# Fc1 of a conditional-experts kernel: one level of the seven-product form for one row, or two levels for two rows with streamed weights

## The chip, the cores and the metric

One core of a Trainium2 chip (trn2) runs the whole kernel. The metric is the device time of one execution in microseconds. A TensorE instruction on fp32 data appears in the profile as two "passes", so one matmul in the code is two matmul instructions in the counts.

## The reference, cut to what matters

```
x: [16, 512, 512]                     # 16 batch rows b, 512 positions, 512 features
h  = gelu(x @ fc1_w.T + fc1_b)        # [16, 512, 2048]
y  = [h @ fc2_w.T + fc2_b  (384 outputs, shared),
      h @ experts_w[idx[b]].T + experts_b[idx[b]]  (128 outputs, one expert for each row)]
x1 = x + y
a  = tanh(x1 @ W1 + b1)               # [16, 512, 128]
s  = a @ v                            # one score for each position
p  = softmax over l of s[l], masked by the row's type: l <= j, l >= j, or l != j
out[j] = x1[j] + (sum over l of p[j, l] x1[l]) / (number of l allowed)
```

## The kernel before, in words

Everything is fp32 and lies transposed: features or hidden units on the 128 partitions, positions along the free axis. A row is split into two halves of 256 positions (HC).

fc1 and fc2 use the seven-product block form: a 2 x 2 block product is made from seven products of sums of blocks. The sums of weight blocks are called s1 to s4, those of the moving side xs (for x) or t1 and in-place sums in hT. Products are called p1 to p7, and the same numbers are the names that fc2 passes to `at(...)`.

- fc1 of a row b is four groups g (`Group`); a group makes 7 products, each of 2 output tiles m and 2 depth chunks k, so 4 matmuls of 128x128 by 128x256. Accumulators are PSUM banks bx, ba, bd and by. After each product one operation on ScalarE (ACT: L294, L300, the Gelu at L285) or on VectorE (DVE: L305, L314) takes its result.
- The 7 weight pieces of a group have two sets of buffers (`pw`, 14 buffers of 256 KB). For the first row the sums are made on DVE and stored to DRAM (`w1s`); later rows load the pieces with SP's queue.
- fc2 of a row is seven products of 16 matmuls (`fc2`). Its shared weights stay in SBUF (fc2_sb, fc2_lo and the sums fc2s); the row's expert is gathered by POOL (GpSimd) and its sums (exs) are made on DVE.
- Then comes `Pooling(b)`: the projection and tanh (L461, L465), the scores (L470), small softmax steps on 32 partitions, coefficients that go to DRAM and come back broadcast (cb), and for each of four chunks of 128 features: weigh (u = x1T times c1), a reversed copy of u on ACT, recur (the scan f at L714), two passes on ACT (v), and finish (two DVE operations into x1T). At last `flip` transposes each chunk into yo (two buffers) and stores it.

The order is written out by hand: each engine executes in the order in which the Python code emits. Pooling of row b runs as a generator beside fc1 and fc2 of row b + 1. Each `yield t` is a cost in us; `slot(budget)` goes on until the budget is used. A negative `yield -n` ends the call and makes the next n - 1 calls of slot do nothing. In fc2, `at("1")`, `at("1b")`, `at("2")` give budgets, `at("5")` runs what is left ("drains"), and `at("7")` and `at("6")` emit two flips each. A name stands behind the emission of the product that it names.

What ends a row in fc2, with the line numbers of the profile:

```
            product(bd, of("a22"), b21, KH, add=True)
            at("4")
            add(out_block(1, 0), bd, u21, ALU.add)     # L387
```

The next row's projection reads all of x1T, so it waits for that add.

Of the kernel before, what the change touches and what calls it, by code (L numbers as in the profile page):

```python
# [17 lines left out]
def tile_cond_experts_then_prompt_pool(  # L18
# [29 lines left out]

    HC = S // 2
    KD = ND // 2  # L50
    KH = NH // 2
    MW = 2 * P
    NG = HID // 2 // MW
    assert NS == 3 and PART == P and ND == 4
# [3 lines left out]
    pw = ctx.enter_context(tc.tile_pool(name="pw", bufs=2 * 7))  # L58
    ps_m = ctx.enter_context(tc.tile_pool(name="ps_m", bufs=1, space=bass.MemoryType.PSUM))
    ps_y = ctx.enter_context(tc.tile_pool(name="ps_y", bufs=1, space=bass.MemoryType.PSUM))  # L60
    ps_l = ctx.enter_context(tc.tile_pool(name="ps_l", bufs=2, space=bass.MemoryType.PSUM))
# [3 lines left out]
    NAMES = ("a11", "a12", "a22", "s1", "s2", "s3", "s4")  # L65
    SUMS = ("s1", "s2", "s3", "s4")
    w1s = {(g, n): dram.tile([P, KD, MW], F32, name=f"w1s_{g}_{n}") for g in range(NG) for n in SUMS}


    todo = []  # L70

    def sums(s1, s2, s3, s4, a11, a12, a21, a22, store=lambda i: None):

        ops = ((s1, a21, a22, ALU.add), (s2, s1, a11, ALU.subtract), (s3, a11, a21, ALU.subtract), (s4, a12, s2, ALU.subtract))

        def one(i):
            nc.vector.tensor_tensor(*ops[i])  # L77
            store(i)

        todo.extend((lambda i=i: one(i)) for i in range(4))  # L80

    def work(n):
        while n and todo:
            todo.pop(0)()
            n -= 1


    def fetch(b, g, queue=nc.sync):
        w = {n: pw.tile([P, KD, MW], F32, tag="w", name=f"w_{b}_{g}_{n}") for n in NAMES}

        def part_of(n):
            r, k = int(n[1]) - 1, int(n[2]) - 1
            return fc1T[:, ts(k, KD), ds(r * (HID // 2) + g * MW, MW)]

        if b:
            for n in ("a11", "s1", "s2", "a12", "s3", "s4", "a22"):
                nc.sync.dma_start(w[n], w1s[g, n] if n in SUMS else part_of(n))
            return w
        a21 = p1.tile([P, KD, MW], F32, tag=("c12", "c21")[g % 2], name=f"a21_{g}")
        for n, t in (("a11", w["a11"]), ("a21", a21), ("a22", w["a22"]), ("a12", w["a12"])):  # L100
            queue.dma_start(t, part_of(n))
        sums(
            *(w[n] for n in SUMS), w["a11"], w["a12"], a21, w["a22"],
            store=lambda i: nc.gpsimd.dma_start(w1s[g, SUMS[i]], w[SUMS[i]]),
        )
        return w

    def load_x(b, queue=nc.sync):
        t = p1.tile([P, ND, S], F32, tag="xT", name=f"xT_{b}")
        for r, c in ((0, 0), (0, 1), (1, 1), (1, 0)):  # L110
            queue.dma_start(t[:, ts(r, KD), ts(c, HC)], xT[b][:, ts(r, KD), ts(c, HC)])
        return t
# [4 lines left out]

    def x_sums(b, xt):
        t = p1.tile([P, 4, KD, HC], F32, tag="tx", name=f"xs_{b}")
        b11, b12, b21, b22 = (block(xt, r, c, KD) for r in (0, 1) for c in (0, 1))  # L120
        ops = ((t[:, 0], b12, b11), (t[:, 1], b22, t[:, 0]), (t[:, 2], b22, b12), (t[:, 3], b21, t[:, 1]))
        return t, [(lambda a=a: nc.vector.tensor_tensor(*a, ALU.subtract)) for a in ops]

    def bank(tag, name, bufs=1):
        return ps_m.tile([P, 2, HC], F32, tag=tag, name=name, bufs=bufs)


    warm = const.tile([P, HC], F32, name="warm")
    nc.vector.memset(warm, 0.0)

    for t in ("ba", "by"):
        warm_ps = bank(t, f"warm_{t}")
        for m in (0, 1, 1):
            nc.tensor.matmul(warm_ps[:, m, :], warm[:, :P], warm, start=(m == 0), stop=True, skip_group_check=True)
# [4 lines left out]
    x_next = load_x(0)  # L139
    w_next = fetch(0, 0, nc.scalar)  # L140
    first_sums = todo[:]
    del todo[:]
    xs_next, x_steps = x_sums(0, x_next)
    for k in range(2):
        x_steps[k]()
        first_sums[k]()
    todo.extend((x_steps[2], first_sums[2], first_sums[3], x_steps[3]))
# [13 lines left out]
    fc2_sb = const.tile([P, NH, 2 * P], F32, name="fc2_sb")  # L161
    fc2_lo = const.tile([P, NH, P], F32, name="fc2_lo")

    def load_fc2(part):
        if part == 0:
            nc.sync.dma_start(fc2_sb, fc2T[:, :, : 2 * P])
        else:
            nc.sync.dma_start(fc2_lo, fc2T[:, :, 2 * P :])

# [4 lines left out]
    nc.vector.tensor_copy(part_f, part)  # L174
    rows = const.tile([P, B], I32, name="rows")
    nc.vector.tensor_scalar(rows, idx_sb, float(P), part_f, ALU.mult, ALU.add)
    onehot = const.tile([E, B], F32, name="onehot")
    nc.vector.tensor_scalar(onehot, idx_sb[:E, :], part_f[:E, :], None, ALU.is_equal)

    def load_expert(b):  # L180
        t = p1.tile([P, NH, PART], F32, tag="exp", name=f"exp_{b}")
        nc.gpsimd.indirect_dma_start(
            out=t.rearrange("p k m -> p (k m)"),
            out_offset=None,
# [715 lines left out]
```

## Time and profile before

| | |
|---|---|
| median of 3 runs | 1669.49 us (1669.25 to 1671.9) |
| the profiled execution | 1669.64 us; span 1667.9 us |
| granted TensorE clock, mean | 0.995 of full speed |
| DMA | 202.40 MB, mean 121 GB/s, 304 GB/s in the first slice of 41.7 us |
| one row, from row start to row start | 101.3 us: fc1 with projection and scores 52.9, fc2 48.4 |
| DVE busy in fc1 / in fc2 of a row | 28.9 of 52.9 us / 22.2 of 48.4 us |
| first product of fc1 | begins 7.72 us after the start |

In a group's row, the number after x is a count of instructions, then come the busy time in us and the mean of one in ns; behind the second bar stands how long the engine was idle before such instructions and what ended the idle time. In a timeline the columns are start, duration, engine, line, operation, output<-inputs, shape; a bracket is the idle time before. In the chain of waits they are start, length and what the chain ran through.

### The profile page before, as it was taken

Reading aid. Unit: us, or ns where it says so; the run is one execution under the profiler, and the core shown is the slowest. Engines: PE = TensorE matmul, PEld = TensorE weight load, DVE = VectorE, ACT = ScalarE, POOL = GpSimd, SP = SyncE. Lnnn points to the kernel's source line nnn. Section 1 sums busy time; section 2 is a strip of 40 time slices with the busy share of each in tenths; the row PEclk is TensorE's granted clock in tenths of the full one; section 3 lists DMA queues with packets and bytes.
Section 4 is the critical chain, followed back from the end, with each engine's and each line's share of the span. In section 5 each row is a group of like instructions: output and inputs, shape, how many; then the busy total and the mean of one; then the engine's idle time right before and its main releaser. Section 6 shows DMA issues by size and latency. Waiting matters only on the chain.

```text
span 1667.9 us, 20795 instructions
## 1 busy us (share of the span) xinstructions
PE 1642.4 (98%) x7428; PEld 1403.3 (84%) x7428; DVE 833.8 (50%) x1560; ACT 559.7 (34%) x1145; POOL 250.9 (15%) x379
## 2 busy tenths in 40 slices
PE   8999999999999999999999999999999999999995
PEld 7888888888888888888888888888888888888884
DVE  3617437273563726527274372735637265272735
ACT  3216044150522506134160441505225061341603
POOL 2001201102020020300202011020200203002020
PEclk9999999999999999999999999999999999999997
DMA  9334353343533335343443534335333353434220
GB/s 304 120 108 133 108 164 102 110 123 109 177 102 108 121 114 152 107 123 99 133 133 108 165 99 113 123 107 180 101 108 120 114 152 108 122 101 133 89 38 26
DMA packets 144359, 202.40 MB, mean 121 GB/s; under 512 B 17008, under 2 KB 104064, under 8 KB 142208
## 3 DMA queue, kind: packets, MB, share of 16 engines
q1 hardware_dynamic: 126160, 150.77, 29.7%
q0 software_dynamic: 14384, 48.63, 10.2%
q10 hardware_dynamic: 3712, 1.67, 0.4%
q8 instruction: 59, 0.97, 0.2%
q14 instruction: 44, 0.36, 0.1%
HBM read 179.89 MB, written 21.06 MB: 120 GB/s over the span
## 4 chain that ended last, share of the span: by engine, by line
PE 97%; DMA 1%; issue 1%; DVE 0%; ACT 0%; POOL 0%; ACTq 0%; POOLq 0%; DVEq 0%
PE bx L259 26%; PE ba L259 20%; PE bd L259 19%; PE bc L259 13%; PE bb L259 7%; PE by L259 7%; PE pa L461 3%; PE psc L470 1%; DMA w_a<-in_fc1T 1%; DMA a<-in_fc1T 0%; PE bd L417 0%; PE pa_last L395 0%; PE be_last L425 0%; DMA expb_sb<-in_exp_b 0%; PE psc_last L409 0%
## 5 line engine op out<-in xcount | busy, mean ns | idle before, releaser
L259 PE MATMUL bx<-xs,w_s 128*128 128x256 f32 x1024 | 242.0, 379 | 0.4 <-ACT ba L294 0.4
L259 PEld LDWEIGHTS bx<-xs,w_s 128*128 128x128 f32 x1024 | 194.5, 190 | 27.2 <-ACT ba L294 0.8
L775 POOL DMA_DIRECT2D out_y<-yo x240 | 154.6, 652 | 213.8 <-DVE yo L772 208.3
L294 ACT COPY ba<-bx 128x512 f32<-128x512 f32 x64 | 36.5, 570 | 399.3 <-PE bx L259 398.8
L305 DVE TENSOR_TENSOR by<-bx,p5s 128x512 f32<-128x512 f32 x64 | 44.8, 700 | 229.6 <-PE bx L259 224.2
L343 ACT ACTIVATE xr<-xr,fc2b_sb 128x256 f32<-128x256 f32 x96 | 43.4, 503 | 319.1 <-DMA xr<-in_xT 298.3
L259 PE MATMUL bx<-xT,w_a 128*128 128x256 f32 x512 | 121.1, 379 | 2.6 <-DMA w_a<-in_fc1T 2.6
L259 PE MATMUL bd<-xs,w_s 128*128 128x256 f32 x512 | 121.1, 379 | 1.7 <-DVE w_s L77 1.7
L259 PE MATMUL ba<-xT,w_a 128*128 128x256 f32 x512 | 122.5, 382 | 0.0
L259 PE MATMUL by<-xT,w_s 128*128 128x256 f32 x512 | 121.0, 379 | 0.0
L259 PE MATMUL bx<-xs,w_a 128*128 128x256 f32 x512 | 120.9, 379 | 0.0
L259 PEld LDWEIGHTS ba<-xT,w_a 128*128 128x128 f32 x512 | 96.0, 190 | 25.4 <-issue 13.0
L259 PEld LDWEIGHTS bd<-xs,w_s 128*128 128x128 f32 x512 | 97.2, 190 | 21.6 <-issue 7.2
L259 PE MATMUL ba<-hT,fc_sb 128*128 128x256 f32 x512 | 113.2, 379 | 0.0
L259 PE MATMUL bb<-hT,fc_sb 128*128 128x256 f32 x512 | 113.1, 379 | 0.0
L259 PE MATMUL bd<-hT,fc_lo 128*128 128x256 f32 x496 | 112.1, 379 | 0.0
L259 PE MATMUL bd<-hT,exp 128*128 128x256 f32 x496 | 112.1, 379 | 0.0
L259 PEld LDWEIGHTS bx<-xT,w_a 128*128 128x128 f32 x512 | 97.1, 190 | 16.4 <-issue 1.7
L259 PEld LDWEIGHTS by<-xT,w_s 128*128 128x128 f32 x512 | 97.3, 190 | 13.2
L259 PEld LDWEIGHTS bb<-hT,fc_sb 128*128 128x128 f32 x512 | 97.3, 190 | 13.2
L259 PEld LDWEIGHTS bx<-xs,w_a 128*128 128x128 f32 x512 | 97.3, 190 | 13.2
L259 PEld LDWEIGHTS ba<-hT,fc_sb 128*128 128x128 f32 x512 | 97.2, 190 | 13.2
(222 smaller groups left out, 2443.4 us busy)
## 6 DMA issues: line engine op xcount, KB each, us to landing
w_s<-w1s_s SPq DMA_DIRECT2D x240, 256.0 KB, 2.7
w_a<-in_fc1T SPq DMA_DIRECT2D x189, 256.0 KB, 3.1
xT<-in_xT SPq DMA_DIRECT2D x64, 256.0 KB, 4.5
xr<-in_xT SPq DMA_DIRECT2D x64, 256.0 KB, 3.1
out_y<-yo POOLq DMA_DIRECT2D x240, 64.0 KB, 2.7
cb<-co_d POOLq DMA_DIRECT2D x15, 769.5 KB, 5.1
w1s_s<-w_s POOLq DMA_DIRECT2D x16, 256.0 KB, 5.8
fc_sb<-in_fc2T SPq DMA_DIRECT2D x1, 2048.0 KB, 14.3
```

The costliest lines, as they stand in the source:

```text
L259: nc.tensor.matmul(bank[:, m, :], w(m, k), mv[:, k, :], start=(not add and m == 0 and k == 0), stop=(k == depth - 1), skip_group_check=True,)
L294: nc.scalar.copy(self.ba, self.bx)
L305: nc.vector.tensor_tensor(self.by, self.bx, self.p5s, ALU.add)
L343: nc.scalar.activation(t[:, m, :], t[:, m, :], AF.Identity, bias=bias)
L461: nc.tensor.matmul(pa, w1_sb[:, dc, :], self.x1T[:, dc, :], start=(dc == 0), stop=(dc == ND - 1))
L470: nc.tensor.matmul(psc, v_sb, self.aT, start=True, stop=True)
L775: nc.gpsimd.dma_start(to[dc, a], yo[ts(a, 32), :].rearrange("j (c i) -> j c i", i=32))
```

## The change

fc1 applies the seven-product form twice, to two batch rows together. The moving operand is 256 columns wide as before: 128 positions of each of the two rows. The weights are cut into blocks of blocks: an outer product (`Outer`, 7 a pair, OUTER order) consists of 7 inner products, each of 4 matmuls with one depth chunk. Every inner product is done in two halves of output tiles (mh), so a pair has 98 steps of 2 matmuls. Partial results of outer products lie in hT and are added up there. hT holds two rows. Then fc2 runs for the two rows one after the other.

All weights, fc1's 49 pieces of a pair and fc2's and the experts' 22 of a row, pass through one ring of ten pieces of 256 KB, loaded by SP in the order of `Ring.plan`; a piece is loaded when the one ten places earlier has been released. fc2's weights no longer stay in SBUF. The sums of fc1's weights are made on DVE during the first pair and stored to DRAM; the sums of x move to POOL (`Moving`), and so do some of the additions into hT.

The pooling of a pair's first row runs in fc2 of the second row; the pooling of the second row runs in fc1 of the next pair and in fc2 of its first row. `slot` now keeps unused or overdrawn credit between calls; the flips are part of the generator, behind a `yield -4`, and are stored by SP. In pooling, u, v and f have one buffer less (u and v one, f two), and the order of the chunks' steps is different.

```
+    RING = 10
-    pw = ctx.enter_context(tc.tile_pool(name="pw", bufs=2 * 7))
+    pw = ctx.enter_context(tc.tile_pool(name="pw", bufs=RING))
...
+    ROOM = ("xr", "yo", "aT", "xr", "yo", "c21")      # temporaries of the first pair's sums
+    def work(n=1):
+        while len(stores) > 5:
+            store_one()
+        while n and todo:
+            load_ahead()                               # the loads of the next three sums
...
+            nc.vector.tensor_tensor(to, in0, in1, op)
+            if store is not None:
+                stores.append((store, to))
...
+    class Ring:
...
+                for r in range(2):
+                    self.plan += [("up", b + r, "a11", h) for h in range(4)]
+                    if r:
+                        self.plan += [("ex", b + r, "a12", h) for h in range(2)]
+                    self.plan += [("up", b + r, "a12", h) for h in range(4)]
+                    self.plan += [("lo", b + r, n, h) for n in LOWER for h in range(2)]
+                    if not r:
+                        self.plan += [("ex", b + 1, "a11", h) for h in range(2)]
...
+        def room(self):
+            return len(self.taken) < RING or self.taken[-RING] in self.free
...
+        def pump(self):
+            while self.at < len(self.plan) and self.room():
...
+                        nc.sync.dma_start(t, w1s[n, h] if (n, h) in w1s else piece1(n, h))
...
+        def release(self, t):
+            if t is not None and t.name.startswith("w_"):
+                self.free.add(t.name)
+            self.pump()
...
+    class Moving:
+        def outer_sum(self, n, eng):
...
+                sub(self.t[:, 1], self.block(0, 1), self.block(0, 0))
+                sub(self.t[:, 0], self.block(1, 1), self.t[:, 1])
...
+        def inner_sums(self, n, eng):                  # four subtractions of 128x256
...
+    class Outer:
...
+        def put(self, bank, r, c, mh, ready=False, eng=nc.vector):
+            src = self.both(bank)
+            for RC, prev, complete in self.to:
+                hc, to = self.place(RC, r, c, mh)
+                if prev is None or ready:
+                    if complete:
+                        self.gelu(hc, to, src)
+                    else:
+                        nc.scalar.copy(to, src)
+                    continue
+                eng.tensor_tensor(to, src, self.place(prev, r, c, mh)[1], ALU.add)
+                if complete:
+                    self.late.append([3 if eng is nc.vector else 5, lambda a=(hc, to, to): self.gelu(*a)])
...
+        def step(self, mh, p):
...
+            if p == 1:
+                u["x"], u["a"] = bank("bx", f"bx_{name}"), bank("by", f"ba_{name}")
+                self.product(mh, u["x"], "a11", o[:, 0, 0])
+                if self.single:
+                    add(self.both(u["a"]), self.both(u["x"]), self.place(self.to[0][1], 0, 0, mh)[1], ALU.add)
+                else:
+                    nc.scalar.copy(u["a"], u["x"])
...
+            elif p == 7:
+                self.product(mh, u["x"], "s3", xi[:, 2], add=True)
...
+                    add(c22, u["x"], u["p5"], ALU.add)
+                    self.put(c22, 1, 1, mh, eng=nc.gpsimd)
...
+        STEPS = ((0, 1), (0, 5), (1, 1), (1, 5), (0, 6), (0, 2), (1, 6), (1, 2), (0, 7), (0, 3), (1, 7), (1, 3), (0, 4), (1, 4))
...
         def slot(self, budget):
             if self.pause:
                 self.pause -= 1
                 return
-            while budget > 0 and not self.done:
+            self.credit += budget
+            while self.credit > 0 and not self.done:
...
                 elif t < 0:
-                    self.pause = -t - 1
+                    self.pause, self.credit = -t - 1, 0
                     return
...
         def run_all(self):
             yield from self.weights()
             yield from self.apply()
+            if not self.last:
+                yield -4
+                for dc in range(ND):
+                    self.flip(dc)
+                    yield 0.7
...
-                    u[dc] = p1.tile([P, 2 * S], F32, tag="u", name=f"u_{b}_{dc}", bufs=2)
+                    u[dc] = p1.tile([P, 2 * S], F32, tag="u", name=f"u_{b}_{dc}", bufs=1)
...
             order = (
-                (weigh, 0), (weigh, 1), (recur, 0), (weigh, 2), (recur, 1), (finish, 0),
-                (weigh, 3), (recur, 2), (finish, 1), (recur, 3), (finish, 2), (finish, 3),
+                (weigh, 0), (recur, 0), (weigh, 1), (finish, 0), (recur, 1), (weigh, 2),
+                (finish, 1), (recur, 2), (weigh, 3), (finish, 2), (recur, 3), (finish, 3),
             )
...
-                nc.gpsimd.dma_start(to[dc, a], yo[ts(a, 32), :].rearrange("j (c i) -> j c i", i=32))
+                nc.sync.dma_start(to[dc, a], yo[ts(a, 32), :].rearrange("j (c i) -> j c i", i=32))
...
+    def drain():
+        while pools:
+            slot(1e9)
+    SPARE = (0.55, 0.35, 0.35, 0.1, 0.35, 0.35, 0.35)   # budget after each step, by outer product
...
+                else:                                    # row == 1, names of fc2's products
+                    if name == "0":                      # between the halves of the first product
+                        pool.project()
+                    elif name == "1":
+                        pool.score()
+                        pools.append(pool)
+                    elif name == "1b":
+                        for h in range(2):
+                            experts.sums("a12", h)
+                    elif name in ("2", "5", "7", "6", "3"):
+                        slot({"2": 5.0, "5": 5.0, "7": 7.0, "6": 6.0, "3": 6.0}[name])
+                    if name == ("4" if b + 1 < B else "3"):
+                        drain()
+                    if more and name == "2":
+                        nxt["x"] = Moving(i + 1)
+                    elif more and name == "6":
+                        nxt["xi"] = nxt["x"].inner_sums(0, nc.gpsimd)
```

In fc1 the projection of the row before stands behind the third step of the first outer product (n == 0, k == 2), its scores behind the ninth.

## The prediction

> **What bounds the kernel now.** I read the page first for its totals and its chain, then the groups, then the chain in time, and at last the timeline around a row's end, where the order of VectorE (DVE) matters.
>
> ```profile
> PE 1642.4 (98%) x7428; PEld 1403.3 (84%) x7428; DVE 833.8 (50%) x1560; ACT 559.7 (34%) x1145; POOL 250.9 (15%) x379
> ...
> PE 97%; DMA 1%; issue 1%; DVE 0%; ACT 0%; POOL 0%; ACTq 0%; POOLq 0%; DVEq 0%
> ```
> ```profile
> 1578.23 1.73 PE bx L259 x8
> 1579.96 6.91 PE ba L259 x32
> ```
>
> TensorE (PE) is the bound and has no holes: 97% of the chain. One fp32 matmul is two instructions, "passes". A product of fc1 is 8 passes in 1.73 us, one of fc2 is 32 in 6.91: 0.216 us a pass in both. (The 379 ns of the groups is one pass with its overlap and is not used.) A row takes 96.8 us for fc1 and fc2 and 4.5 us for its projection and scores.
>
> ```profile
> L714 DVE TENSOR_TENSOR_SCAN f<-cb,u 128x512 f32<-128x512 f32 x60 | 73.2, 1219 | 3.9 <-ACT u L706 3.9
> ...
> L732 ACT ACTIVATE v<-f,U,cb 128x512 f32<-128x512 f32 x60 | 48.5, 809 | 14.2 <-DVE U L730 14.2
> L305 DVE TENSOR_TENSOR by<-bx,p5s 128x512 f32<-128x512 f32 x64 | 44.8, 700 | 229.6 <-PE bx L259 224.2 <-ACT hT L285 5.4
> ...
> L726 DVE TENSOR_TENSOR x1T<-x1T,f 128x512 f32<-128x512 f32 x60 | 41.5, 692 | 2.1
> L719 DVE TENSOR_TENSOR f<-v,cb 128x512 f32 x60 | 41.0, 683 | 0.0
> L772 DVE STREAM_TRANSPOSE yo<-x1T 128x512 f32<-128x512 f32 x60 | 40.7, 698 | 42.5 <-DMA out_y<-yo 42.5
> ...
> L733 ACT COPY v<-v 128x512 f32<-128x512 f32 x64 | 39.6, 618 | 2.0
> L706 ACT ACTIVATE u<-u 128x512 f32<-128x512 f32 x60 | 37.5, 625 | 0.5
> ```
>
> These are the pooling of the row before, which runs beside PE. See that it is a chain over two engines: scan on DVE, two passes on ScalarE (ACT), two more on DVE. The transposes have already waited 42.5 us for their two buffers.
>
> ```profile
> 716.69 1.89 PE L259 MATMUL bx<-xT,w_a 128*128 128x256 f32 x8
> 716.89 0.69 DVE L387 TENSOR_TENSOR x1T<-bd,u 128x512 f32<-128x512 f32 x1 [6.21 <-PE bd L259]
> ...
> 718.41 3.60 PE L461 MATMUL pa<-x1T,w_sb 128*128 128x512 f32 x8
> ```
>
> The end of a row: DVE, idle for 6.21 us, writes the last block of x1T (L387), and PE reads x1T in the projection (L461) one product later. This hand-over is what the change puts work in front of.
>
> **PE: what is saved.** Before, a pair of rows has 2 x 4 groups x 7 products x 4 = 224 matmuls in fc1. After it has 49 products of 4 matmuls, also 256 columns wide: 196. Over 8 pairs 224 matmuls go, 448 passes x 0.216 = **-96.8 us**. fc2, projection and scores keep theirs. A product is now 4 passes, 0.864 us, and fc1 of a pair 98 of them, 84.6 us.
>
> **DVE and ACT in fc1.** Evacuations of a pair on DVE: 4 in the first outer product, 10 in the second and third, 16 in the fourth, 10 in each of the last three: 70. Adds back to back start 0.61 us apart (1614.59, 1615.20, 1615.80 in the timeline; 0.70 is a duration with overlap): 43 us. Experts' sums are 8 x 0.61 = 5 us, the pooling of the pair's second row about 22. That is 70 of 84.6 us. It fits, but in the second and third outer products 6.1 + 4.9 budgeted + 1.2 = 12.2 us stand against 12.1, and an accumulator must be read within three products (2.6 us).
>
> GpSimd (POOL) gets the sums of x and 14 adds of 128x512 a pair. The trace of before has no such row: its POOL tensor operations are 128x4. The GPSIMD Engine Reference (section 3.1, side-by-side cycle accounting) gives 4497 ns on GpSimd and 2293 on DVE for a two-input add of 2048. The trace has 2282 ns for DVE's at 128x2048 (L354), so I scale DVE's 0.68 us by 1.96: an estimate of 1.3 us for 512, 0.7 for 256, 2.4 for 1024. POOL: 14 x 1.3 + 28 x 0.7 + 4 x 2.4 = 48 us a pair, and it fits. Against the change speaks the page SBUF — State Buffer (Who interferes with whom): a DVE operation with both inputs in SBUF is shut out while a GpSimd operation reads SBUF. Evacuations read PSUM and are free of it; some 26 pooling and expert operations of 0.6 us and more are not. With POOL busy 57% of the time and half an operation (0.65 us) to wait, that is 26 x 0.57 x 0.65 = 10 us more on DVE. By the trace alone, where POOL never computes, it is 0. Ends: 0 and 10 us a pair (DVE loses x's sums, but it is no bound, so no gain). I take 3, since DVE has slack over the pair and not in its second and third product: 7 x 3 = **+21 us**.
>
> **The end of a pair.** fc2's seven products stay 6.91 us each. In the pair's second row, the first row's pooling gets steps only at "2", "5", "7", "6", "3", and a pause of n swallows n-1 calls. "2" runs the small steps down to `yield -2`; "5" is swallowed; "7" runs the rest down to `yield -6`; "6" and "3" are swallowed; "4" drains all that is left: the whole of apply() and the four transposes. "4" stands ahead of `add(out_block(1, 0), ...)`, and DVE is in order. So that work is between the sixth product's add and the row's last. With u and v at one buffer and the new order, a chunk is scan 1.22 + U 0.25 + v 0.81 + copy 0.62 + f 0.68 + x1T 0.69 = 4.27 us, one after the other. Four of them and the first weighing (0.68 + 0.63) are 18.4. POOL's x_max add 0.4. Transposes: two, then the third waits for the first one's four stores, now on SP: 4 x 0.45 to issue (SP's x loads took 0.49 each) + 2.7 to land (page, out_y). The fourth likewise, so 7.7 in all. Last the add, 0.69. From the sixth product's end that is 0.9 + 18.4 + 0.4 + 7.7 + 0.7 = 28.1 us. The seventh product covers 6.9, three products of the next pair 2.6; then PE's projection waits for x1T: 18.6 us. Behind it wait all of PE's products, and with them ACT and DVE.
>
> The clock adds to it. In the tail of before, after 7.4 us without PE work:
>
> ```profile
> 1657.68 0.43 PE y_bd L487 x2
> ...
> 1661.10 0.43 PE y_bd L487 x2
> 1661.53 0.23 PE y_by L487 x2
> ```
>
> Two passes take 0.43 us for 4.4 us, then 0.23: 2.2 us lost. TensorE: Matmul & The Clock Gate (Part 1) has half rate after an idle window of about 3.4 us and full rate after as long a busy one, so 1.7 us a stall. The trace decides: 2. Per pair 20.6 us; for the 7 pairs that have a next one **+144 us** (by the page's figure +142, without the gate +130). Ends: 14 us if ACT's steps overlap better and the stores land faster, 25 if SP's small stores are slow. At the very end the drain stands at "3", ahead of the sixth product's add. DVE begins 2.7 us after the fifth product, is through with the last two adds 30.2 after it, where before PE went on 8.0 after it: 22.2 + 2 = **+24 us** (16 to 30).
>
> **The start.** SP first issues 16 loads of x (16 x 0.49 = 7.9 us), and only then the first weights, which before came by ACT's queue; the first product, at 7.72 us before, comes about 6 later. The first pair loads about 55 pieces of 256 KB for sums and raw blocks, stores 48, and loads 8 pieces' worth of experts and expert sums and 2 MB of x: 30 MB. At the 304 GB/s of the first slice, where the DMA engines were 9 tenths busy, 99 us against 84.6 of PE. 14 + 6 = 20, and SP's loads queue behind stores that wait for DVE and behind six temporaries: I take **+25** (10 to 45).
>
> **Streaming later** costs nothing while its cover holds: a pair has 49 + 44 pieces, 24 MB, and the whole kernel about 280 MB, 160 GB/s. Seven pieces lie ahead of the three in use, 12 us of fc1 or one whole product of fc2 (6.9 us), against 2.7 us to land. The 16 x loads (8 us on SP) come when the ring already holds the row's last ten pieces. If SP were held by a wait of DVE's for longer than that, each microsecond would be PE's. The transposes' stores are such a wait, but PE stands then anyway.
>
> **Sum.** The profiled execution took 1669.64 us (span 1667.9), 0.15 over the median. 1669.6 - 96.8 + 21 + 144 + 24 + 25 = **1787 us**.
>
> **Rivals.**
> - *The drain does not hold PE* (the other side): the calls at "6" and "3" move enough of apply() ahead, or it runs under the seventh product. Then 1669.6 - 96.8 + 21 + 25 = 1619. For it: DVE is 46% busy in fc2 (22.2 of 48.4 us in the windows), so room exists. Against: the pauses leave the calls nothing, and the row's last add is behind the drain. It decides at (96.8 - 46) / 8 = 6.4 us per boundary. 0.11.
> - *DVE becomes the bound of fc1 as well*: POOL's lock and the 12.2 against 12.1 cost 10 us a pair, not 3: 1836. For it: the three-product limit; against: the first outer product gives 7 us back. 0.15.
> - *Streamed weights come late in every pair*: SP, in order, held by stores and residual loads; SP already waits 268 us for p1x in the waits of SP's queue. With 6 us a pair more, 1829. 0.10.
> - *PE's passes do not stay at 0.216* in groups of four, 0.235 say: 3136 x 0.019 = 60 us, 1847. Against: 8 and 32 passes cost the same each. 0.04.
> - My forecast: 0.60.
>
> **How the numbers follow.** All low ends give 1669.6 - 96.8 + 98 + 16 + 10 = 1697, all high ends (70 in fc1) 1669.6 - 96.8 + 175 + 30 + 45 + 70 = 1893. A range of 1690 to 1865 leaves out the first rival and the far end. A measurement of this kernel tells 0.2% (3.3 us) from no change. Faster is the first rival and a little of mine with a boundary under 6.4 us: 0.12; same 0.01; slower 0.87.
>
> **What would show it.** PE's passes fall by 448 to about 6980. In the chain, DVE, ACT and DMA pieces between the last product of each odd row and the projection, some 19 us, seven times, and a slice of PE at 7 or 8 tenths there. L387's counterpart comes about 21 us after the seventh product, with the transposes just before it, waiting for out_y. PE at half clock for some 4 us after. In the first 120 us SP waits and DMA at 9 tenths. It is wrong if the projection follows the third product at once, or if PE's idle time lies inside fc1.

## The result, and the profile after

| | before | after |
|---|---|---|
| median of 4 runs | 1669.37 us (1668.74 to 1671.9) | 1995.32 us (1991.35 to 1999.94) |
| profiled execution, span | 1669.64, 1667.9 us | 1996.06, 1994.2 us |
| granted TensorE clock, mean | 0.995 | 0.914 |

The change makes the kernel slower: 1.195 times the time before, 95% interval 1.1921 to 1.1979. The forecast was 1787 us with a range to 1865. The direction was right, the size was not: 209 us are missing in the sum.

The page first: its busy times, and PE's and the clock's rows of the 40 slices.

```profile
PE 1652.7 (83%) x6980; PEld 1359.6 (68%) x6980; DVE 1147.5 (58%) x2030; ACT 596.9 (30%) x1225; POOL 487.2 (24%) x503
...
PE   6779967898689968899688996889967899688956
...
PEclk8889978999799988899899997999978999789987
```

PE has 6980 instructions, 448 fewer, as the blocks of fc1 say. At 0.216 us they are worth 96.8 us. But its busy time went up by 10.3, from 1642.4 to 1652.7: the passes that are left cost more, and the clock row shows why, with a 7 or 8 wherever PE's row dips to 7 or less. Idle time went from 25.5 to 341.5 us. (In the trace after, the chain of waits loses its thread early: its PE share is 7% of the span, so I read stages and waits instead.)

Who made PE wait, from the list of waits (us in total, times, longest):

```profile
PE pa L752 <- DVE x1T L677: 137.6, 7, 19.9
...
ACT cb L975 <- DMA cb<-co_d: 119.6, 15, 10.3
...
ACT v L1033 <- DVE U L1028: 103.9, 53, 3.1
...
PE bd L516 <- ACT p L571: 93.8, 31, 5.2
...
DVE yo L1073 <- DMA out_y<-yo: 78.1, 30, 7.1
```

The first line is the wait that was forecast, seven times, 19.7 us each. The second, third and fifth are waits inside the pooling, on ACT and DVE. The fourth was not forecast: PE, in the middle of fc1, waits 31 times for ACT to copy the bank `bd` of product 5. It was a risk that the prediction named only for DVE.

The forecast wait in the timeline, at the end of an odd row, ahead of pair 3 (pairs are counted from 0; start and duration in us; in brackets, the engine's idle time before and who ended it):

```profile
720.94 3.62 PE L618 MATMUL bd<-hT,w_lo_a 128*128 128x256 f32 x16
721.14 0.69 DVE L673 TENSOR_TENSOR x1T<-bc,u 128x512 f32<-128x512 f32 x1 [4.42 <-PE bc L618]
721.75 0.68 DVE L1003 TENSOR_TENSOR u<-x1T,cb 128x512 f32<-128x512 f32 x1
...
740.88 1.30 DVE L1073 STREAM_TRANSPOSE yo<-x1T 128x512 f32<-128x512 f32 x2 [0.40 <-POOL x1T L1058]
...
741.62 11.61 SPq L1076 DMA_DIRECT2D out_y<-yo  x16
...
747.73 0.71 DVE L1073 STREAM_TRANSPOSE yo<-x1T 128x512 f32<-128x512 f32 x1 [5.54 <-DMA out_y<-yo]
...
750.56 0.71 DVE L1073 STREAM_TRANSPOSE yo<-x1T 128x512 f32<-128x512 f32 x1 [2.12 <-DMA out_y<-yo]
...
751.19 0.65 DVE L677 TENSOR_TENSOR x1T<-bd,u 128x512 f32<-128x512 f32 x1
751.90 3.78 PE L752 MATMUL pa<-x1T,w_sb 128*128 128x512 f32 x4 [19.58 <-DVE x1T L677]
```

Between the sixth product's add (L673) and the row's last (L677) stand 30 us: the whole of apply(), from 721.75 to 740.8, and four transposes, of which the third and fourth wait for the stores of the first two. The projection's first half, which needs only the blocks of x1T that are ready, ran at 730.44; the second half begins at once after L677.

And the wait that was not forecast, twice in the same pair's fc1. The second part is there to show what follows such a stall.

```profile
800.78 1.04 ACT L975 COPY cb<-cb 128x1024 f32<-128x1024 f32 x1 [9.76 <-DMA cb<-co_d]
801.73 0.58 ACT L566 COPY ba<-bx 128x512 f32<-128x512 f32 x1
...
802.24 0.58 ACT L571 COPY p<-bd 128x512 f32<-128x512 f32 x1
...
802.87 1.60 PE L516 MATMUL bd<-xi,w_f_s_s 128*128 128x256 f32 x4 [4.71 <-ACT p L571]
```
```profile
830.21 4.08 ACT L533 ACTIVATE hT<-hT,fc1b_sb 128x256 f32<-128x256 f32 x10
...
834.20 0.56 ACT L571 COPY p<-bd 128x512 f32<-128x512 f32 x1
...
834.81 2.07 PE L516 MATMUL bd<-xi,w_f_s_s 128*128 128x256 f32 x4 [2.78 <-ACT p L571]
836.68 1.91 PE L516 MATMUL bx<-xi,w_f_s_s 128*128 128x256 f32 x4
838.39 1.91 PE L516 MATMUL ba<-xT,w_f_s_a 128*128 128x256 f32 x4
840.09 1.45 PE L516 MATMUL bx<-xi,w_f_s_s 128*128 128x256 f32 x4
841.38 1.03 PE L516 MATMUL ba<-xT,w_f_s_a 128*128 128x256 f32 x4
```

At 800.78 ACT stands in its order on the pooling's copy of `cb`, 9.76 us idle for a DMA, with PE's copies behind it. At 830.21 it works through ten Gelus that were held back, and PE's copy is the eleventh. The stall of 2.78 us is followed by four products at about half rate: from 834.81 to 841.38 are 6.57 us where four products take 3.46. So this stall cost 5.9 us, not 2.8. Pair 3 is not typical in this: in five of the seven later pairs the same wait was followed by products at full rate, as in pair 1:

```profile
357.34 1.13 PE L516 MATMUL bd<-xi,w_f_s_s 128*128 128x256 f32 x4 [2.79 <-ACT p L571]
358.31 1.03 PE L516 MATMUL bx<-xi,w_f_s_s 128*128 128x256 f32 x4
```

Where the 326.3 us between the spans lie, by the stages of PE's timeline. fc1 of the seven later pairs lasts 135.2 to 140.0 us each, 963.7 together, against 84.6 of products and 4.5 of projection and scores in each (623.7):

| | forecast | measured |
|---|---|---|
| passes saved | -96.8 | -96.8 |
| fc1 of seven pairs over its products, without the wait for x1T | +21 | +202 (118 idle, 85 slow passes) |
| wait for x1T at the end of seven pairs | +130 (and 14 of clock) | +138 (its clock is in the row above) |
| very end | +24 | +25 (22.9 idle, 2.4 of clock) |
| first pair: later start, and over its products | +25 | +56 (8 and 48) |
| fc2 (102.3 us a pair, 101.4 in the first) | 0 | +5 |
| sum | +117 | +329 |

340.0 less 137.6 is the 202; its parts are the idle times in those stages (255.2 - 137.6 = 118) and the rest. By the granted clock in the trace PE was busy at half rate for 132 us of these stages, so 66 of the 85 us are the clock; the other 19 stay open. The sum closes to 3 us. Nearly the whole error is in the second row (202, where 21 and 14 of clock had been put: 167), and 31 are in the first pair.

### The profile page after: what moved, and what is told of

Its sections match the earlier page's. It is cut to its first block, busy times and chain, and to the rows that moved or that the text cites. A ratio compares the mean times of both kernels' runs of the same rounds, so it can differ in the third digit from the quotient of the medians.

```text
span 1994.2 us, 22032 instructions
## 1 busy us (share of the span) xinstructions
PE 1652.7 (83%) x6980; PEld 1359.6 (68%) x6980; DVE 1147.5 (58%) x2030; ACT 596.9 (30%) x1225; POOL 487.2 (24%) x503
## 5 line engine op out<-in xcount | busy, mean ns | idle before, releaser
L546 POOL TENSOR_TENSOR hT<-c,hT 128x512 f32<-128x512 f32 x112 | 148.6, 1339 | 283.4 <-DVE c L585 282.3
L533 ACT ACTIVATE hT<-hT,fc1b_sb 128x256 f32<-128x256 f32 x416 | 173.4, 495 | 59.0 <-DVE hT L546 58.4
L752 PE MATMUL pa<-x1T,w_sb 128*128 128x512 f32 x120 | 68.2, 709 | 137.6 <-DVE x1T L677 137.6
L516 PE MATMUL bx<-xi,w_f_s_s 128*128 128x256 f32 x512 | 146.1, 411 | 11.4 <-issue 6.3
L516 PEld LDWEIGHTS bx<-xi,w_f_s_s 128*128 128x128 f32 x512 | 106.3, 210 | 34.6 <-issue 16.7
L618 PE MATMUL bb<-hT,w_up_a 128*128 128x256 f32 x512 | 117.0, 383 | 3.8 <-DMA w_up_a<-in_fc2T 3.6
L618 PEld LDWEIGHTS bb<-hT,w_up_a 128*128 128x128 f32 x512 | 95.2, 190 | 28.4 <-issue 9.4
L618 PE MATMUL ba<-hT,w_up_a 128*128 128x256 f32 x512 | 114.5, 379 | 0.0
L618 PE MATMUL bd<-hT,e 128*128 128x256 f32 x496 | 112.1, 379 | 0.0
L516 PE MATMUL bx<-xi,w_f_a_s 128*128 128x256 f32 x384 | 107.7, 406 | 2.8 <-DVE by L575 2.8
L618 PEld LDWEIGHTS ba<-hT,w_up_a 128*128 128x128 f32 x512 | 97.2, 190 | 16.6 <-issue 3.8
```

The source lines that it names most:

```text
L516: nc.tensor.matmul(bank[:, m, :], w[:, ts(2 * mh + m, P)], mv, start=(not add and m == 0), stop=True, skip_group_check=True,)
L533: nc.scalar.activation(to[:, m], src[:, m], AF.Gelu, bias=fc1b_sb[:, hc + m : hc + m + 1])
L546: eng.tensor_tensor(to, src, self.place(prev, r, c, mh)[1], ALU.add)
L618: nc.tensor.matmul(bank[:, m, :], w(m, k), mv[:, k, :], start=(not add and m == 0 and k == 0), stop=(k == depth - 1), skip_group_check=True,)
L752: nc.tensor.matmul(pa, w1_sb[:, dc, :], self.x1T[:, dc, :], start=(dc == 0), stop=(dc == ND - 1))
```

## The experiments

All are edits of the changed kernel, some of a version that came before. Times are medians; the kernel before took 1668.7 to 1670.2 beside them.

**The order at the end of a pair.** The row's last addition goes ahead of the drain.

```diff
-            at("4")
             add(out_block(1, 0), bd, u21, ALU.add)
+            at("4")
```

> The changed kernel with one line moved: in fc2 the row's last add into x1T stands ahead of the call at "4", so the drained pooling comes behind it on VectorE. If the drain's place in VectorE's order makes the stall (my prediction), the projection no longer waits 19.6 us seven times; but VectorE is still busy with the drain until some 21 us after the last product, the next pair's first adds (product 6) come that late, and PE has only about 11 us of other work: the wait moves there and is halved, about 10 us and a shorter cold phase, so 7 x 10 = 70 us less, about 1925 us. If something else holds x1T (the seventh product's accumulator, SP's stores), nothing moves: 1995.

2005.1 us (1998.4 to 2011.8): no gain. PE no longer waits for x1T, but:

```profile
PE bd L516 <- ACT p L571: 186.5, 38, 13.2
PE bx L516 <- issue: 48.0, 14, 6.8
```

The wait for ACT's copies rises from 93.8 to 186.5 us. The drained steps are on ACT too, in order, ahead of the next pair's first copies. Freed from DVE's order, PE runs into ACT's: in pair 3 it waits 12.96 us for a copy that ACT reaches when apply() is through, and then 6.28 us more (listed under "issue") for an addition behind the transposes, which wait for their stores.

**The pause for the coefficients.** The pooling in fc1 asks for `cb` six calls after its DMA; six calls now are six products of 0.86 us and were of 1.73. Twelve for odd rows.

```diff
-            yield -6
+            yield -12 if b % 2 else -6
```

> The changed kernel; in the pooling of odd rows (the one beside fc1) the pause behind the coefficients' load is 12 calls instead of 6. New theory (ScalarE's order): a call now comes every 0.86 us instead of 1.73, so after 6 calls the load of cb has not landed, ScalarE stands 9.8 us at the reversed copy of cb, the copy of product 5 out of its only bank waits behind it and PE 4.7 us plus a cold phase of about 2: 7 x 6.7 = 47 us less, 1948 us, and that wait is gone from PE's list. Rival (VectorE is what is short in fc1): the time comes back as waits for VectorE's adds a few steps later: 1985 or more.

1998.2 us, no gain. In pair 3 ACT's wait for `cb` falls from 9.76 to 1.44 us, and the waits on the copy stay at 13.0 us, with other lengths (5.83, 4.13, 3.01). The copy now stands behind other work: before the wait of 5.83 us ACT is idle 3.60 us for DVE's U, then does v and six Gelus.

**The Gelus.** Late Gelus are no longer all run at an outer product's end; they run from the fourth step of the next one, behind the copies of product 5.

```diff
-                op.tick()
+                if k >= 3:
+                    op.tick()
...
-            op.tick(all=True)
+            if n == 6:
+                op.tick(all=True)
```

> The changed kernel; the Gelus still open at the end of an outer product are not emitted there but after the next one's fourth step, so both copies of product 5 come first on ScalarE. ScalarE's order theory: PE's waits of 1.5, 2.8 and 4.1 us at the beginning of the last three outer products go, with the cold phases behind them (about 5): 7 x 13 = 91 us less, about 1904 us. Rival (VectorE or GpSimd late, the Gelus only follow them): PE then waits for VectorE's adds in the same places, and no more than 20 us are gained: 1975.

1981.65 us. The wait on the copy falls from 13 to about 8 us a pair, and new ones of 1.7 (DVE by) and 1.2 (POOL xi) take part of it back. So the bursts of Gelus are some 5 of the 13.

**GpSimd's reads.** Where GpSimd makes sums of x, it now only writes zeros, so fc1's input sums are left out.

```diff
-            sub = lambda *a: eng.tensor_tensor(*a, ALU.subtract)
+            sub = lambda *a: eng.memset(a[0], 0.0)
...
-                eng.tensor_tensor(to, in0, in1, ALU.subtract)
+                if eng is nc.gpsimd:
+                    eng.memset(to, 0.0)
+                else:
+                    eng.tensor_tensor(to, in0, in1, ALU.subtract)
```

> The changed kernel with GpSimd's sums of x replaced by memsets of the same tiles (the sums of x are left out from the first outer product on). GpSimd then writes but does not read there. If GpSimd's reads shut VectorE out (the page's lock), VectorE's small operations of up to 2.40 us beside a 128x1024 sum go back to 0.2, the wait of 2.2 us for hT in the third outer product and its cold phase go, and f and es of 1.2 to 1.7 us go back to 0.7: 7 x 5 to 8 us, 1940 to 1960. If the long VectorE operations have another cause, they stay and the time is 1995 within 5.

1960.1 us, 35 less. What it removes is seen in the timeline of the changed kernel:

```profile
778.90 2.40 DVE L911 TENSOR_SCALAR nd<-pos,wt 32x16 f32<-32x16 f32 x1
778.92 2.35 POOL L261 TENSOR_TENSOR xT<-xT 128x1024 f32<-128x1024 f32 x1
...
782.74 1.51 PE L516 MATMUL bx<-tx,w_f_s_a 128*128 128x256 f32 x3 [2.23 <-DVE hT L546]
```

A DVE operation on 32x16, 0.22 us where nothing runs beside it, takes 2.40 beside GpSimd's 2.35, and PE's wait of 2.23 us follows; in this run that wait is 0.50. The Trainium skill has such a lock in SBUF — State Buffer (Who interferes with whom): the two engines share a pair of ports, and whoever issues first holds it for the whole instruction. But it is not GpSimd's reads alone: with memsets, which only write, the same operation is still held:

```profile
762.88 0.95 POOL L261 MEMSET xT<- 128x1024 f32 x1
762.88 1.98 DVE L914 TENSOR_SCALAR nd<-pos,wt 32x16 f32<-32x16 f32 x1
```

DVE's operations with two inputs in SBUF did go back when the reads went: f (L1017) from 863 ns on average to 688, es (L430) from 866 to 685. The memsets are also shorter than the sums (0.95 us against 2.35), so the run doesn't tell the lock from GpSimd's time. The prediction had put 21 us on the lock in the seven later pairs. Of the 35 us measured, 26 lie in their fc1 and 7 in the first: the size was near and the place right.

**No pooling in fc1.** The odd row's pooling is projected and scored as before, but all its further steps are given to the calls in the next row's fc2 (SPARE is 0, pauses are 1 or 2, drain at "3").

```diff
-    SPARE = (0.55, 0.35, 0.35, 0.1, 0.35, 0.35, 0.35)
+    SPARE = (0, 0, 0, 0, 0, 0, 0)
...
-                    elif name == "7":
-                        drain()
+                    if name in ("0", "1", "2", "5", "6"):
+                        slot({"0": 5.0, "1": 4.0, "2": 1.0, "5": 6.0, "6": 6.0}[name])
+                    elif name == "3":
+                        drain()
```

> The changed kernel with the pooling of odd rows taken out of fc1: no budget beside fc1, all of it in fc2 of the next pair's first row (5, 4, 1, 6, 7, 6 us at its calls, pauses made to fit). Theory now: pooling's own steps on ScalarE (v, u, cb) wait for VectorE or a DMA in fc1, and the copies of product 5 queue behind them; longer pauses only swapped one such wait for another. Without pooling in fc1 PE's waits for product 5's copy fall from 13 us a pair to the Gelu burst alone, 3 to 5, with less cold time: 8 to 10 us and as much clock, 7 x 15 = 105 us less, about 1890. VectorE's load in fc2 of row 0 is 22 + 24 of 48 us, so nothing new should stand there. Rival (single bank of product 5 and Gelu bursts are enough by themselves): 13 stays near 10, 1960.

1893.3 us (1890.4 to 1896.2), 102 less.

```profile
PE pa L752 <- DVE x1T L677: 141.7, 13, 20.0
PE bd L618 <- DVE p L662: 29.8, 7, 5.0
...
PE bd L516 <- ACT p L571: 15.1, 24, 1.3
```

The wait on the copy goes from 93.8 to 15.1 us, and fc1 of a later pair from 137.5 to 115 us on average, of which 19.7 is the untouched wait for x1T. Without that wait, fc1 was 29 us a pair over its products and is now 6. So 23 of the 29 us are the pooling's. The gain is not larger because fc2 pays: its eight pairs take 57 us more, 43 of it idle, most of that in the wait for p57 (29.8 us, second line) and for tanh (11.3 us).

**Both.** The even row's pooling is also taken apart: budgets at the odd row's calls, the rest in the first outer product of the next fc1, and the additions into x1T are placed ahead of the calls; the Gelus as above. The pooling of the odd row is as in the version before.

```diff
-                    if name == ("4" if b + 1 < B else "3"):
+                    if name == "3" and b + 1 == B:
                         drain()
...
-                if n or k > 12:
-                    slot(SPARE[n])
+                if n == 0:
+                    slot(0.6)
```

> All remedies together: pooling of odd rows only in fc2 of the next row, of even rows in fc2 of theirs with shorter pauses and its rest in the next pair's first outer product, the adds into x1T ahead of the calls, and the open Gelus after the next outer product's fourth step. If the hand-over at a pair's end (19.6 us, now 2 to 4 expected) and ScalarE's order (13 us) are the losses, with their cold phases about 45 of the 50 us that a pair has over PE's own time go: 1995 - 7 x 42 - 10 at the end = about 1690, close to the 1669 of before; what is left is the first pair (56 us over PE's time). If VectorE itself is short, PE's waits for its adds come up instead and the time stays above 1800.

1766.8 us (1761.4 to 1772.2). fc1 of a regular pair is down to 95, 6 over its products, projection and scores; fc2 is up to 110 to 115 from 102, PE waiting for DVE's p57 (L664 there, 30.1 us) and for the tanh (21.7 us), which stands on ACT behind residuals that wait for their loads.

**Warm clock.** Twenty matmuls of 512 columns whose results are overwritten run while PE waits for x1T, seven times.

```diff
+            for _ in range(20 if b % 2 else 0):
+                nc.tensor.matmul(pa, w1_sb[:, 0, :], w1_sb.rearrange("p k a -> p (k a)"), start=True, stop=True)
```

> The changed kernel with 20 matmuls of 512 columns (17.3 us, results overwritten) on TensorE ahead of the odd rows' projection, so that it works while it waits for x1T. If a stall costs its length and a cold phase of about 2 us behind it (my prediction's term), the time falls by 7 x 2 = 14 us, to 1981, and the projection's first passes take 0.43 us each, not 0.85. If the clock were no part of it: 1995.

1988.1 us (1985.3 to 1990.9), 7 less, 1 us a stall; the intervals of the two ratios overlap (1.187 to 1.1951 here). The clock was not kept, though:

```profile
731.81 17.33 PE L752 MATMUL pa<-w_sb 128*128 128x512 f32 x40
748.98 1.88 PE L754 MATMUL pa<-x1T,w_sb 128*128 128x512 f32 x4
753.18 3.19 PE L754 MATMUL pa<-x1T,w_sb 128*128 128x512 f32 x4 [2.32 <-DVE x1T L677]
```

A wait of 2.32 us was left, and the projection's second half took 3.19 us where the first took 1.88. So this run doesn't show what a warm clock is worth. The trace of the changed kernel does: after its seven long waits the granted clock was 0.50 for 3.3 to 6.1 us with PE busy, 33.8 in all, so 17 us were lost, 2.4 a stall. Of the 66 us that half clock costs in these fc1, some 49 are left for the shorter stalls.

**The start.** All of fc1's weight pieces are loaded raw; none is summed or stored.

```diff
     def start_piece(o, n):
         key = ("f1", 0, o, n)
+        t = ring.tiles[key] = ring.tile(key)
+        nc.sync.dma_start(t, raw1(o, n))
+        return True
...
```

> All 49 weight pieces of every pair's fc1 are loaded raw from the weights as given (the pieces that need sums take the a11 block instead, so fc1's result is not the reference's); the 40 sums of weight pieces on DVE, their loads into temporaries and their stores in the first pair are left out. The sums for fc2 stay. If the first pair's 48 us over its ideal come from making the pieces (SP's in-order queue of loads and stores, 40 x 0.6 = 24 us of DVE), the first fc1 falls from 132.6 us to about 97 and the time from 1995 to about 1960. Rival: the first pair is slow for the same reason as the others (ACT's order, the accumulators' evacuations), then it loses only the 10 us of waits for weights and the time is about 1985.

1977.9 us (1968.0 to 1983.1). The first fc1 takes 111.2 us, not 132.6: 21 of the 48 us are the pieces. The forecast of 97 was too good: 27 remain, although no pooling runs beside the first fc1. The longest wait of PE there, 7.61 us, follows DVE's wait of 7.59 us for the store of a sum for fc2, which this edit leaves in; another, 3.00 us, is for ACT's copy.

**The repair, tuned.** From the version "both": additions that free accumulators in fc2 are ahead of the pooling's steps, the bias steps of the residuals follow where their loads have landed, the last row's transposes are behind its additions, and the first weights are loaded after a quarter of x.

```diff
-        at("5")
         p5x = tmp("u2", f"p5x_{b}")
         add(p5x, bc, xr22, ALU.add)
         xr21 = residual(1, 0)
+        biased(xr12, 0)
+        at("5")
+        biased(xr21, 1)
         product(bd, of("s3"), b12, KH)
-        at("7")
         p57 = tmp("u3", f"p57_{b}")
         add(p57, bd, p5x, ALU.add)
+        at("7")
```

> Beside e8_pooling_in_fc2 (1766.8): the additions that free PE's accumulators in fc2 stand ahead of the pooling's steps, the residuals' bias steps on ACT stand where their loads have landed, the last row's transposes go behind its additions, and the first weights are loaded after the first quarter of x. If what e8 still lost in fc2 (110 to 115 us a pair against 101) is the order on DVE and ACT alone, fc2 falls to about 102 a pair: 7 x 9 = 63 us, the tail's wait of 22.8 us to about 10, the start by 3: 1766 - 63 - 13 - 3 = about 1687. If it is DVE's load in fc2, the waits reappear at the next product and it stays above 1740.

1706.1 us, still 1.0238 times the time before (1.0206 to 1.0271), and the best of all versions.

```profile
PE 1586.8 (93%) x6980; PEld 1321.6 (78%) x6980; DVE 1169.3 (69%) x2030; ACT 595.9 (35%) x1225; POOL 486.4 (29%) x503
```

The same 6980 passes take 66 us less of PE than in the changed kernel: that is the clock (0.976). fc2 is back at 101.4 to 102.2 us a pair, so it was the order there, not DVE's load. What is left over the products: 692.4 - 623.7 = 69 us in seven fc1, 134.9 - 84.6 = 50 in the first, 15.2 at the end. Together 134 against 97 saved, which is the 37 us that it lacks.

**Stores of the pieces.** The same with prepared pieces stored after two further sums.

```diff
-        while len(stores) > 5:
+        while len(stores) > 2:
```

> e11_tuned with the prepared pieces' stores issued after two further sums rather than five. If DVE's 8 us wait for a store before it can take the next room (first pair) is this, the first pair is 5 to 8 us shorter than e11_tuned's. Rival: SP, in order, then waits for DVE earlier and the loads come later by as much: no change or a few us slower.

1709.8 us, ratio 1.0245 (1.0228 to 1.0262): no difference to the version before it. The 7.47 us wait in the first pair becomes 4.52, and others take its place; the rival holds.

**A step further.** Fewer pooling steps ahead of the odd row's last additions, more behind them; the last row's apply() behind PE's last additions; the second half of fc2's pieces in `cb`'s room.

```diff
-  slot({..., "7": 6.0, "6": 6.0, "3": 3.5}[name])
+  slot({..., "7": 6.0, "6": 3.5, "3": 3.5}[name])
...
-                    slot(0.6)
+                    slot(0.7)
```

> Beside e11_tuned (1706.1): fewer pooling steps ahead of the odd row's last additions (PE waited 1.9 to 3 us a pair at its second product, with about 1 us of cold clock after it: 7 x 3.5 = 24 us), the last row's pooling behind PE's last additions instead of ahead of them (15.2 us to about 5: 10 us), and the second half of fc2's prepared pieces in a room of its own, so that DVE doesn't wait for stores in the first pair (about 10 of its 50 us). Expected 1706 - 24 - 10 - 10 = about 1662, under the kernel before (1669.3). If fc1's remaining loss is GpSimd's hold on DVE's SBUF operations, which this leaves alone, fc1 stays at 98 a pair and the time at about 1685.

1736.4 us, 30 more than the tuned version. The wait that it aimed at goes (16.7 us, listed under "issue"), and two others come:

```profile
PE bx L525 <- DMA w_f_s_s<-w1s_s_s: 39.2, 7, 6.0
PE bd L525 <- ACT p L580: 17.1, 7, 2.7
```

Steps moved back by 2.5 us of budget end in the next fc1, where ACT's copy is late again; and streamed weights are late for the first time, 5.6 us a pair. That fits the transposes' stores on SP (in order, 16 issues in 11.61 us) now lying ahead of those loads. This was not tried by itself. The other two edits gave 4 us in the first pair and 3 at the end.

**The copy on DVE.** Is it ACT, or any engine that also carries the pooling?

```diff
-                nc.scalar.copy(u["p5"], bd)
+                nc.vector.tensor_copy(u["p5"], bd)
```

> The changed kernel with the copy of product 5's bank on DVE (14 of 0.6 us a pair) and not on ACT; nothing else differs. If the 13 us a pair come from ACT's own queue (Gelus and pooling steps ahead of the copy), they go, and DVE's longer queue gives back some 3 us: 7 x (10 + 4 of cold clock) = 98 us less at best, about 1920. Rival: what counts is that an in-order engine shared with the pooling frees a bank that exists once; then the wait appears under DVE's name with about the same size (over 8 us a pair), and the time stays within 1970 to 2000.

1997.9 us (1995.1 to 2001.3), no change.

```profile
PE bd L516 <- DVE p L571: 81.0, 40, 5.9
...
PE bx L516 <- issue: 17.5, 5, 4.5
```

The wait moves with the copy. It is not ACT's order alone: DVE's queue, which carries pooling steps too, frees the bank about as late. One of the waits under "issue" (3.42 us, in pair 3) ends with ACT's copy of `bx` (L566), which still stands behind `cb`.

**More distance.** In the order of steps one product, 0.86 us, lies between the two uses of `bd`, and the copy alone takes 0.58. Three products between them:

```diff
-        STEPS = ((0, 1), (0, 5), (1, 1), (1, 5), (0, 6), (0, 2), (1, 6), (1, 2), ...
+        STEPS = ((0, 1), (0, 5), (1, 1), (0, 6), (0, 2), (1, 5), (1, 6), (1, 2), ...
```

> The changed kernel with the two halves of product 5 further apart: the order of an outer product's first steps is (0,1) (0,5) (1,1) (0,6) (0,2) (1,5) (1,6) (1,2). Before, one product of 0.86 us lay between the two that use the single bank bd, and the copy alone takes 0.58; now three lie there, 2.6 us. If the 13 us of waits in fc1 (4.71, 1.45, 2.78 and 4.07 in pair 3) are this missing slack, each falls by 1.73: to 3.0, 0, 1.1 and 2.3, 6.4 a pair, with some 3 us of half clock less: 7 x 9.5 = 66 us, about 1930. Rival: the copy is late by whatever DVE and ACT have ahead of it, and with the copy out of the way the next accumulator's release (product 6's or 2's) is as late: PE waits as long under another name, and the time stays at 1985 to 2000.

1990.05 us (1985.5 to 1992.25), 5 less; the intervals of the two ratios overlap.

```profile
PE bx L516 <- issue: 48.0, 17, 4.5
PE bx L516 <- POOL xi L278: 25.0, 14, 2.2
...
PE bd L516 <- ACT p L571: 14.1, 7, 2.0
```

The copy's wait falls to 14.1 us, and PE waits about as long one or two steps on. For `bx` the profile names no releaser; in pair 3 such a wait (3.64 us) ends at 809.71, just after ACT's copy of `bx` (L566, to 809.61), again behind `cb`. The waits for sums of x come from the edit itself: GpSimd is through with the second sum 4.8 us after an outer product's start, as in the changed kernel (840.44 after 835.68; 834.05 after 829.28), but PE now needs it one product sooner. The rival holds: the bank was only the first thing to be late. With the same order in the tuned version, and the two edits of the step further that had helped:

> e11_tuned (1706.1) with that order of steps, with the last row's pooling behind PE's last additions and the second half of fc2's prepared pieces in a room of its own (both from e13_best, where they gave 2 and 4 us), and the pooling's steps at their calls as in e11_tuned. Expected 1695 to 1702; under 1690 only if the order of the steps also takes away part of fc1's 9 us a pair over its products.

1735.7 us, 30 more than the tuned version. The sums of x (`xi`) cost 23.2 us in all, where they cost 7.7, and the streamed weights 15.7, where they cost 7.5. Distance gained in one place is taken from another.

## Why the prediction was wrong, step by step

- *PE, what is saved: right.* 6980 passes, and 0.216 us each wherever the clock is full.
- *The end of a pair: right.* Forecast 18.6 us of wait, measured 19.7; L677 ended 30.9 us after the sixth product (720.94 to 751.84), where 28.1 had been worked out, and the steps between stand in the order written down. Two small errors nearly cancel: the transposes took 10.4 us where 7.7 had been summed, and half of the projection ran ahead of the wait. What was not seen is that the wait stands twice: undone on DVE, it comes back on ACT (the first experiment).
- *The very end: right,* 22.2 against 22.9, for the reason given (PE waits for the last row's addition behind the drain).
- *DVE and ACT in fc1: the step that failed.* The working added DVE's work in a pair, 70 of 84.6 us, and concluded that it fits. For ACT it gave no sum at all. The average was right (in pair 3's fc1 DVE is busy 89.4 and ACT 56.9 of 137.7 us), but it doesn't decide. An accumulator has to be freed within one to three products, 0.9 to 2.6 us, and ahead of its release in the same in-order queue may stand a pooling step that itself waits, `cb` for a DMA (9.76 us) or v for U (up to 3.1), or a burst of ten Gelus (4.08). I named the limit of three products but compared it with loads only, and missed that for `bd` it is one product. Term: +21 forecast, +202 measured; with the pooling out of fc1 it falls from 29 us a pair to 6. The prediction's own sign of being wrong, PE idle inside fc1, is what the trace shows.
- *The clock: mis-sized by its count.* 2 us a stall was near for the long ones (2.4), but only eight were counted, 16 us. The seven later fc1 lost 66 us to half clock, some 49 of it after shorter waits: those of 2.2, 4.1 and 4.4 to 5.2 us in every pair, that of 2.8 in two of the seven. The passes of the whole kernel cost 107 us more than at 0.216 (10.3 + 96.8).
- *GpSimd's hold on DVE: right in kind.* 3 us a pair forecast; leaving GpSimd's sums out gained 26 us in seven pairs, 35 in all, GpSimd's own time among it.
- *The start: half seen.* +25 forecast, +56 measured: 21 of it the pieces, the later start 8 (forecast 6). Of the other 27, one stall of 7.61 us lies behind the sums for fc2; the rest was not taken apart.
- *Streamed weights: right* for this kernel (the two lines on weights in fc1 and fc2 come to 13.3 us, most of it at the start), and no longer so in two of the repaired ones.
- *The rivals:* "DVE becomes the bound of fc1 as well" had the place, at a price of 10 us a pair; 29 were found, and DVE is not the bound (65% busy in pair 3's fc1): the wait moves to whichever engine frees the accumulator. The copy on DVE shows it.

What stays open: how the 29 us a pair divide between the order on DVE and that on ACT. Every single release that was made early showed the next one late, so the shares can't be told apart by such edits; only the removal of the pooling took most of it away. What holds the 6 us a pair that remain was not tested by itself.

## What to carry to other kernels

When products get shorter, compare each accumulator's time to its next use with the longest chain that may stand ahead of its release in an in-order queue, waits included, not the engines' sums with each other. Work that fitted between long products (here the pooling beside 8 passes a product) may not fit between short ones (4), even if nothing is added to it; a pause counted in products halves with them. And a fused block form saves passes only as long as PE stays fed: the 97 us saved here are 12 in each of eight pairs, less than the 17 us a pair (118 in seven) that PE stood idle in fc1 beside the long wait.

## What the runs showed of the hardware

- In pair 3 a wait of 2.78 us was followed by half rate for 6.13 us (granted clock 0.50 from 834.11 to 840.94). The same wait was followed by half rate in two of the seven later pairs and by a granted clock of 1.00 in five; a wait of 2.22 to 2.23 us in the third outer product was followed by half rate in all seven (mean granted clock 0.59 to 0.66 in the 5 us from its end). So the length of a wait alone does not decide. In the tuned version a wait of 3.63 us was followed by one product at nearly full rate (1.10 us) and then about two at 1.70 and 1.91. The Trainium skill (TensorE: Matmul & The Clock Gate, Part 1) speaks of an idle window of about 3.4 us; these waits show that a shorter one can be enough, and that the loss may begin late.
- GpSimd held a small DVE operation (32x16, 0.22 us alone) for 2.40 us with a subtraction of 128x1024, and for 1.98 us with memsets of 128x1024 and 128x256, which read nothing.
- GpSimd's add of 128x512 took 1339 ns on average; 1.3 us had been estimated from DVE's.
- Sixteen stores of a transposed row's pieces held SP's queue for 11.61 us, and the first buffer was free 5.54 us after DVE was ready for it.
